# Gate and up products of six of eight token blocks as seven half-size products, with four FFN banks and a down product taken pair by pair

## Chip, cores and metric

One NeuronCore of a Trainium2 chip runs the whole program. The metric is device time in microseconds (us), as the median of several executions. Profiles are one execution each, recorded by the hardware profiler.

## What is computed

The input x has 4 sequences of 1024 tokens with 512 channels. The reference does this (weights come as arguments, `ternary` rounds a matrix to -1, 0, 1 times its mean magnitude):

```
xn  = layernorm(x)
# attention: 16 heads of 32, decayed linear attention in chunks of 128 tokens
q, k, v = split(rmsnorm(xn, qkv_norm_w) @ ternary(qkv_w).T)
per chunk:  o = scale * ((q k^T * mask) v + (q * lam_t) S);  S = lam_T * S + (k * lam_rev)^T v
att = rmsnorm(rmsnorm(o, norm_w), proj_norm_w) @ ternary(proj_w).T
# FFN, hidden size 2048
ffn = (silu(xn @ w_gate.T) * (xn @ w_up.T)) @ w_down.T
out = x + att + ffn
```

## The kernel before

The 4096 tokens are cut into eight blocks b = 0 to 7 of 512 tokens. Every float32 factor of a product is split into two float16 halves, hi and lo, and a product is the sum of hi·hi, hi·lo and lo·hi, so each product of 128 contracted channels costs three matmuls (with exact ternary weights only two).

The FFN of a block works on the hidden size in 16 slices j of 128, in two halves of 8 slices. `ffn_up` makes one slice: for gate and then for up, 4 channel groups times 3 matmuls with 512 moving columns (tokens), 12 matmuls into one PSUM bank of pool `ps_f` (3 banks). ScalarE (ACT) takes the silu of the gate bank (line 852); VectorE (DVE) multiplies the up bank with it (line 855); ACT rounds the result to its hi half (line 879), and GpSimd (POOL), or DVE for the last slices of a half, makes the lo half (line 880). Two slices share one tile `ghl` and one scale, and are called a pair below. After 8 slices, `ffn_down` makes the four token chunks one after the other, each with 24 matmuls of 512 columns into one bank, with down weights that stay in SBUF (tiles `wda` and `wdb`). DVE adds the bank to `acc` (line 905). Gate and up weights are converted to hi and lo once, in block 0, kept in DRAM as `gu_d`, and read again in each later block, 512 KB for a slice, four slices ahead (`load_gu`).

Block 0 has another loop (`ffn0`), in which the weights are converted while they are used.

The attention of a block is made in two halves of 256 tokens (`att_half`), a coroutine with some 30 yields. In its course: four steps of q and k products (16 matmuls of 256 columns with the weights `wqkT`), two of v, then eight steps with scores (4 matmuls, into one of the two banks of pool `ps_s`, evicted by DVE in line 680, split by ACT in 684 and POOL in 685), the products with v four steps later (`intra`, evicted by ACT in 702 and DVE in 704), the state S (DVE, 732 and 739), norms (among them line 770 on DVE), and the projection.

The main loop has 48 steps for each block. In a step it issues one FFN piece (in blocks 1 to 7, 12 matmuls of 512 columns, 2.6 us of TensorE), then one yield of each attention half under way, then the pieces that `later(...)` has put down for this step: a list FIRST, which runs at the head of a step, and a list LAST, which runs at its end. `in_order` chains the instructions of DVE, ACT, POOL and SyncE (SP) in this written order, so that each of those engines works strictly through its list; TensorE's (PE's) order is the program's as well. `ln_plan` puts the layernorm of block b+1 into the last third of block b: loads, statistics, scaling on ACT, then the hi half on ACT, the lo half on POOL (line 479) and a transposing DMA into `xT`, four of them for a block. `place` picks the step of a few loads by how many bytes are due around it. All but one small DMA are issued by SP, in one queue.

Of the kernel before, what the change touches and what calls it, by code (L numbers as in the profile page):

```python
# [20 lines left out]
XS = 2.0**10  # L21
# [7 lines left out]
def block_kernel(ctx, tc, x, qkv_w, qkv_nwT, proj_w, proj_nwT, proj_nw, norm_w, s, w_gu, w_down, out):  # L29
# [17 lines left out]
    ps_f = ctx.enter_context(tc.tile_pool(name="ps_f", bufs=3, space=bass.MemoryType.PSUM))  # L47
    ps_s = ctx.enter_context(tc.tile_pool(name="ps_s", bufs=2, space=bass.MemoryType.PSUM))
# [92 lines left out]
    gu_d = dram.tile([P, NJ * 2048], F16, tag="gu_d", name="gu_d")  # L141
# [9 lines left out]
    ones = pnw_bc[:, :P]  # L151
# [9 lines left out]
    def t32():  # L161
        return wt([P, 512], F32, "t32", 10)
# [46 lines left out]
    def load_x(c, tag="xin", bufs=4):  # L209
        xt = wt([P, C], F32, tag, bufs)  # L210
        SY.dma_start(xt, xf[c * P : (c + 1) * P, :])
        return xt
# [50 lines left out]
    def tern_scale(src, count, col):  # L263
        n = len(src)
        a = asum[:, col : col + n]
        for i in range(n):
            with after(pin):
                sumabs(i, src[i], a[:, i : i + 1])
            if i % 2:
                yield  # L270
        r1 = ct([P, 1], F32, f"r1_{col}")
        V.tensor_reduce(r1, a, AX.X, ALU.add)
        yield
        yield
        sc = tsc[col]
        V.tensor_scalar(sc[:, 0:1], col_sums(r1, 1), 1.0 / count, 1e-5, ALU.mult, ALU.max)
        V.tensor_scalar(sc[:, 1:2], sc[:, 0:1], 0.5, None, ALU.mult)
        V.tensor_scalar(sc[:, 2:3], sc[:, 0:1], -0.5, None, ALU.mult)
# [58 lines left out]
    def raw_pair(g, kind):  # L337

        if kind == 2:
            return [t32(), t32()]  # L340
        if g == 0 and kind == 0 or g % 2:
            t = wt([P, 2, C], F32, *(("ghl", 4) if g else ("kn", 1)))
            return [t[:, 0, :], t[:, 1, :], t]
        return [wt([P, C], F32, *(("xin", 4) if g else ("xn2", 2))) for _ in range(2)]
# [29 lines left out]
    def group_scale(g, kinds=(0, 1, 2)):  # L374


        m = gq.pop((g, kinds))
        o = om[:, g, kinds[0] : kinds[-1] + 1]
        oi = o.bitcast(I32)
        V.tensor_scalar(o, col_sums(m, len(kinds)), 2.0**-64, 2.0, ALU.max, ALU.mult)  # L380
        V.tensor_scalar(oi, oi, 24, 23, ALU.logical_shift_right, ALU.logical_shift_left)
        V.tensor_scalar(oi, oi, -1.0, float(204 << 23), ALU.mult, ALU.add)
        gs = slice(g, g + 1)
        if 0 in kinds:
            inverse(ug[:, gs], o[:, 0:1], 1 / XS)
            V.tensor_scalar(bsc0[:, gs], o[:, 0:1], 2.0**-30 / XS, None, ALU.mult)
        if 2 in kinds:
            V.scalar_tensor_tensor(cg[:, gs], om[:, g, 1:2], om[:, g, 2:3], bsc0[:, gs], ALU.mult, ALU.mult)
            inverse(icg[:, gs], cg[:, gs], 1 / XS)

# [4 lines left out]

    def group_conv(g, r, kinds=(0, 1, 2)):
        j = 2 * g + r
        if 0 in kinds:
            gu0[j] = gu = wt([P, 2, 2, CC, P], F16, "gu", 4)
        for kind in kinds:  # L400
            src, w1 = raw.pop((g, kind, r)), om[:, g, kind : kind + 1]
            if kind < 2:
                hi, lo = (gu[:, kind, n].rearrange("p c q -> p (c q)") for n in range(2))
            else:
                if g not in wd:
                    wd[g] = wd_tile(g // (NG // 2))
                hi, lo = (wd[g][:, r, n, :] for n in range(2))
            la = A.activation(hi, src, AF.Copy, scale=w1)
            if kind == 0 or g == 0 and kind == 1 or g <= 1 and kind == 2:
                lv = V.scalar_tensor_tensor(lo, src, w1, hi, ALU.mult, ALU.subtract)  # L410
            else:
                if kind == 1:
                    G.tensor_scalar(src, src, w1, None, ALU.mult)  # L413
                else:
                    A.activation(src, src, AF.Copy, scale=w1)
                lg[0] = G.tensor_tensor(lo, src, hi, ALU.subtract).ins  # L416
        if 0 in kinds:
            SY.dma_start(gu_d[:, j * 2048 : (j + 1) * 2048], gu.rearrange("p a b c d -> p (a b c d)"))
            return la.ins, lv.ins
# [15 lines left out]
    def ln_stats0():  # L435
# [16 lines left out]
        G.tensor_scalar(rs[:, 2, :], rs[:, 1, :], QS, None, ALU.mult)  # L452
# [21 lines left out]
    def ln_chunk(b, k):  # L474
        xts = lnst[b][1]
        xT = blk[b][0]
        xn2 = wt([P, 2 * C], F16, "xn2", 2).rearrange("p (a c) -> p a c", a=2)
        A.copy(xn2[:, 0, :], xts[k])  # L478
        G.tensor_tensor(xn2[:, 1, :], xts[k], xn2[:, 0, :], ALU.subtract)  # L479

        def turn():
            SY.dma_start_transpose(
                xT[:, :, :, k * P : (k + 1) * P].rearrange("p a c t -> p (a c) t"),
                xn2.rearrange("p a c -> p (a c)"),
            )

        return turn

    def ln_plan(b, end):
# [37 lines left out]
        def split(k):  # L527
            if k == 0:
                blk[b] = [wt([P, 2, CC, HB], F16, "xT", 1), None, rs]
            turns[k] = ln_chunk(b, k)  # L530

        turns = {}
        first, lo = b == 1, 0
        for k in range(4):
# [3 lines left out]
            else:  # L538
                lo = place(max(lo, e - 12), e, 0.7, lambda k=k: load(k))
            later(end - (10 - k // 2 if first else 18 - k), lambda k=k: stats(k), last=True)  # L540
            later(end - (6 - k // 2 if first else 12 - k), lambda k=k: scaled(k), last=True)
            later(end - ((5, 5, 3, 3) if first else (9, 8, 5, 4))[k], lambda k=k: split(k), last=True)
            later(end - ((4, 4, 2, 2) if first else (7, 6, 4, 3))[k], lambda k=k: turns[k]())
# [23 lines left out]
    def att_half(b, half):  # L567
        _, h, rs = blk[b]
# [52 lines left out]
        for k in range(2):  # L621
# [6 lines left out]
            vhl = wt([P, 2 * C], F16, "vhl", 5).rearrange("p (h a d) -> p h a d", a=2, d=D)  # L628
# [119 lines left out]
        def norms(u):  # L748
# [5 lines left out]
            o2, u.o3 = t32(), t32()  # L754
# [19 lines left out]
            if u.g < B * N // P - 2:  # L774
                on = wt([P, 2 * C], F16, "vhl", 5).rearrange("p (a c) -> p a c", a=2)
                oT = wt([P, 2 * C], F16, "vhl", 5).rearrange("p (a c t) -> p a c t", a=2, t=P)
# [64 lines left out]
    def ffn_up(b, j, gu, bs, done):  # L841
        xT = blk[b][0]
        xhi, xlo = xT[:, 0], xT[:, 1]
        for kind in range(2):
            pm = bank(ps_f)
            for c in range(CC):
                T.matmul(pm, gu[:, kind, 0, c, :], xhi[:, c, :], start=(c == 0), stop=False)
                T.matmul(pm, gu[:, kind, 0, c, :], xlo[:, c, :], start=False, stop=False)
                T.matmul(pm, gu[:, kind, 1, c, :], xhi[:, c, :], start=False, stop=(c == CC - 1))
# [3 lines left out]
            else:  # L853
# [4 lines left out]
                if b or j >= NJ - 4:  # L858
                    later(1, lambda: load_gu(NJ * b + j + 4))
            yield  # L860

    def load_gu(q):

        if q >= NB * NJ:
            return
        j = q % NJ
        gus[q] = gu = wt([P, 2, 2, CC, P], F16, "gu", 4)
        SY.dma_start(gu.rearrange("p a b c d -> p (a b c d)"), gu_d[:, j * 2048 : (j + 1) * 2048])

    gus = {}  # L870

    def plain(gts, late=NJ):


        def done(j, gf):
# [4 lines left out]
            (V if j > late else G).tensor_tensor(ghl[:, 1, :], gf, ghl[:, 0, :], ALU.subtract)  # L880
# [3 lines left out]
    def ffn_down(b, k, g0, gts, c):  # L884
# [29 lines left out]
    def load_acc(b, k):  # L914
        g = 4 * b + 2 * k
        acc[g // 2] = wt([P, 2, C], F32, "acc", 4)
# [3 lines left out]
    def ffn(b):  # L920
        for hh in range(2):
            js = range(hh * NJ // 2, (hh + 1) * NJ // 2)
            gts = []
            done = plain(gts, js[-4])
            for j in js:
                yield from ffn_up(b, j, gus.pop(NJ * b + j), bsc, done)
            for k in range(4):
                yield from ffn_down(b, k, js[0] // 2, gts, c2[:, hh : hh + 1])

    def ffn0():  # L930
        prev = None

        def down(ks):
            g, gts = prev
            for k in ks:
                for _ in ffn_down(0, k, g, gts, icg[:, g : g + 1]):
# [56 lines left out]
    masks((0, 1))  # L993
# [10 lines left out]
    def prep():  # L1004
        with after(pin):
            masks((2, 3))
        qw = load_rows(qkv_w, ("qst", "kst", "qhl", "khl"))
        SY.dma_start(nw_bc, norm_w.partition_broadcast(P))
        yield from prep_qkv_w(qw)

    def prep_proj():
        pw = []
        for r in range(2):
            t = wt([P, 2, C], F32, "acc", 4)
            SY.dma_start(t, proj_w[2 * r * P : 2 * (r + 1) * P, :].rearrange("(n p) c -> p n c", p=P))
            pw += [t[:, 0, :], t[:, 1, :]]
# [11 lines left out]
    mh.update({at[2 * b] + 7: (b, 1) for b in range(NB)})  # L1028
# [3 lines left out]
    for n in at:  # L1032
        for i, size in ((2, 1.3), (3, 2.0), (4, 1.3), (5, 2.0), (6, 4.0), (24, 2.0), (25, 2.0)):
            moved[n + i] = moved.get(n + i, 0) + size
    for b in range(1, NB):
        for i in range(0, TS, 2):
            if i % 24 < 16:
                moved[t0[b] + i] = moved.get(t0[b] + i, 0) + 1.3
        for i in (7, 6, 4, 3):
            moved[t0[b] - i] = moved.get(t0[b] - i, 0) + 2.0  # L1040
        for k in range(2):
            lo = max(at[2 * b - 2] + 12, t0[1] + 9) + k
            place(lo, max(lo + 4, t0[b] + 12), 1.3, lambda b=b, k=k: load_acc(b, k))
    side, side2 = prep(), prep_proj()
    t = 0
    for b in range(NB):
        if b + 1 < NB:
            ln_plan(b + 1, TS)
        for i, _ in enumerate(ffn(b) if b else ffn0()):
            for _ in range(int(0.8 * t) - int(0.8 * (t - 1))):  # L1050
                next(side, 1)
            if t == 12 or 28 <= t < 34 or 36 <= t < 56 and t % 2:
# [15 lines left out]
            if b == 0 and i == TS - 1:  # L1068
                half_scales(0)
                half_scales(1)  # L1070
                in_order(keep=False)
            run_due(FIRST)
# [59 lines left out]
```

## Time and profile before

| | |
|---|---|
| median of 3 executions | 1350.65 us (1350.37 to 1351.06) |
| profiled execution, its own time | 1351.69 us |
| its span, first to last instruction | 1348.7 us |
| busy, share of the span | PE 98%, DVE 52%, ACT 41%, POOL 46% |
| mean granted clock of PE | 0.997 |
| DMA | 178.10 MB, mean 132 GB/s; main queue busy for 47.9% of 16 engines' span |

The page names instruction groups by line, engine, operation, output and inputs, with the count, the busy time in us, the mean duration of one in ns, and after the bar the idle time of the engine just before them. Matmuls overlap each other, so the mean duration of one (381 ns for 512 columns) is its latency; what a matmul costs in a stream is the distance from one to the next, which is read from the timeline. A busy time with such overlap is a little over the sum of the distances.

### The profile page before, as it was taken

To read this page: it belongs to the slowest core of one execution; us is meant where nothing else is said; L and a number is where in the kernel's file an instruction comes from. 1 tells how busy PE (TensorE), PEld (TensorE's weight loads), DVE (VectorE), ACT (ScalarE), POOL (GpSimd) and SP (SyncE) were. 2 spreads that over 40 slices of the span, in tenths; PEclk is the share of its full clock that TensorE was granted. 3 is DMA by queue.
4 is the path that set the end of the run, shared out by engine and by line. 5 is a ranking of instruction groups with operands and counts; after the bars stand their busy time and mean duration, and the time that the engine had idled before them with its cause. 6 is when DMAs were issued, how large, how long until landed. Compare 5 with 4: busy or idle time off the path is not lost.

```text
span 1348.7 us, 21547 instructions
## 1 busy us (share of the span) xinstructions
PE 1318.9 (98%) x8514; PEld 695.3 (52%) x8514; DVE 701.0 (52%) x1228; ACT 557.0 (41%) x1061; POOL 619.1 (46%) x648
## 2 busy tenths in 40 slices
PE   4999999999999999999999999999999999999998
PEld 2444555555555555554555555554555555555554
DVE  7898744546343553537443364545534445446442
ACT  5846544244433344334433244433524235344341
POOL 3656753355424454435544254534635244544351
PEclk9999999999999999999999999999999999999999
DMA  9644637156371736335463636445372636444420
GB/s 342 244 155 149 187 90 198 59 148 148 89 194 32 187 95 168 114 102 129 101 170 95 157 110 134 116 123 129 94 171 88 156 102 157 104 130 112 110 63 32
DMA packets 156037, 178.10 MB, mean 132 GB/s; under 512 B 101664, under 2 KB 101664, under 8 KB 155936
## 3 DMA queue, kind: packets, MB, share of 16 engines
q1 hardware_dynamic: 155792, 176.73, 47.9%
q8 instruction: 66, 1.08, 0.3%
q14 instruction: 35, 0.29, 0.1%
q10 hardware_dynamic: 144, 0.01, 0.0%
HBM read 119.55 MB, written 33.55 MB: 114 GB/s over the span
## 4 chain that ended last, share of the span: by engine, by line
PE 88%; DVE 5%; DMA 2%; POOL 2%; issue 1%; ACT 1%; POOLq 0%; DVEq 0%; ACTq 0%; SPq 0%
PE psf L112 65%; PE psa L112 20%; PE pss L112 2%; DMA gu_d<-gu 1%; DVE acc L905 1%; DVE gs L366 1%; DMA xin<-in_x_dram 1%; DVE h L562 0%; POOL gu L416 0%; POOL ghl L413 0%; DMA t<-in_w_down_dram 0%; DMA xin<-in_w_gu_dram 0%; DVE t L288 0%; POOL xin L413 0%; DVE t L855 0%
## 5 line engine op out<-in xcount | busy, mean ns | idle before, releaser
L112 PE MATMUL psf<-xT,gu 128*128 128x512 f16 x3072 | 704.9, 381 | 5.8 <-DVE t L855 2.8
L112 PEld LDWEIGHTS <-gu 128*128 128x128 f16 x3072 | 294.6, 98 | 334.1 <-issue 11.0
L685 POOL TENSOR_TENSOR t<-t,t 128x512 f16<-128x512 f32 x128 | 150.5, 1177 | 186.5 <-ACT t L684 186.1
L112 PEld LDWEIGHTS <-ghl 128*128 128x128 f16 x1536 | 146.9, 98 | 163.6 <-issue 1.6
L880 POOL TENSOR_TENSOR ghl<-t,ghl 128x512 f16<-128x512 f32 x86 | 101.8, 1183 | 222.4 <-ACT ghl L879 221.9
L879 ACT CAST ghl<-t 128x512 f16<-128x512 f32 x128 | 79.0, 617 | 285.6 <-DVE t L855 285.5
L112 PE MATMUL psf<-wdb,ghl 128*128 128x512 f16 x768 | 175.5, 379 | 1.7 <-DVE acc L905 1.0
L112 PE MATMUL psf<-wda,ghl 128*128 128x512 f16 x768 | 175.7, 379 | 0.0
L855 DVE SCALAR_TENSOR_TENSOR t<-psf,bsc,t 128x512 f32<-128x512 f32 x128 | 95.9, 749 | 123.1 <-PE psf L112 114.4
L852 ACT ACTIVATE t<-psf,ug 128x512 f32<-128x512 f32 x128 | 87.5, 684 | 123.4 <-PE psf L112 123.2
L680 DVE SCALAR_TENSOR_TENSOR t<-pss,rs,mask 128x512 f32<-128x512 f32 x128 | 95.5, 746 | 77.7 <-PE pss L112 73.9
L684 ACT CAST t<-t 128x512 f16<-128x512 f32 x128 | 78.8, 616 | 115.4 <-DVE t L680 114.8
L112 PE MATMUL psa<-h,wqkT 128*128 128x256 f16 x1024 | 122.2, 273 | 1.4 <-DVE S L732 1.4
L112 PEld LDWEIGHTS <-wqkT 128*128 128x128 f16 x1024 | 99.8, 98 | 25.4 <-issue 1.6
L905 DVE SCALAR_TENSOR_TENSOR acc<-psf,c,acc 128x512 f32<-128x512 f32 x56 | 42.1, 751 | 69.1 <-PE psf L112 68.9
L644 POOL TENSOR_TENSOR t<-t,t 128x512 f16<-128x512 f32 x28 | 33.5, 1198 | 79.2 <-ACT t L643 79.1
L781 POOL TENSOR_TENSOR vhl<-t,vhl 128x512 f16<-128x512 f32 x30 | 35.5, 1182 | 64.7 <-ACT vhl L780 64.6
L112 PEld LDWEIGHTS <-t 128*128 128x128 f16 x1040 | 47.6, 96 | 32.1
L631 DVE SCALAR_TENSOR_TENSOR vhl<-psa,rs,vhl 128x512 f16<-128x512 f32 x32 | 24.0, 751 | 74.8 <-ACT vhl L630 68.6
L112 PE MATMUL psa<-wvT,h 128*128 128x512 f16 x256 | 60.5, 379 | 1.3 <-DVE S L732 1.3
L479 POOL TENSOR_TENSOR xn<-xin,xn 128x512 f16<-128x512 f32 x28 | 32.7, 1169 | 59.3 <-ACT xn L478 59.1
L706 POOL TENSOR_TENSOR t<-t,t 128x512 f32<-128x512 f32 x28 | 38.8, 1385 | 45.8 <-DVE t L704 45.8
(202 smaller groups left out, 1402.7 us busy)
## 6 DMA issues: line engine op xcount, KB each, us to landing
gu<-gu_d SPq DMA_DIRECT2D x112, 512.0 KB, 3.7
qst<-sd SPq DMA_DIRECT2D x48, 256.0 KB, 4.3
kst<-sd SPq DMA_DIRECT2D x48, 256.0 KB, 4.4
xin<-in_x_dram SPq DMA_DIRECT2D x32, 256.0 KB, 4.4
acc<-in_x_dram SPq DMA_DIRECT2D x16, 512.0 KB, 4.8
gu_d<-gu SPq DMA_DIRECT2D x16, 512.0 KB, 4.0
sd<-qhl SPq DMA_DIRECT2D x16, 512.0 KB, 2.9
sd<-khl SPq DMA_DIRECT2D x16, 512.0 KB, 3.5
```

The lines of the kernel that those rows point to most:

```text
L112: tc.keep_in_program_order(nc.tensor.matmul(*a, **k))
L644: G.tensor_tensor(vrl, vr, vrh, ALU.subtract)
L680: V.scalar_tensor_tensor(sm, pss, u.rk, mask[:, 4 * qd : 4 * qd + 4, :], ALU.mult, ALU.mult)
L684: A.copy(smh, sm)
L685: G.tensor_tensor(sml, sm, smh, ALU.subtract)
L706: later(1, lambda: G.tensor_tensor(u.o, u.o, u.oc, ALU.add), last=True)
L781: G.tensor_tensor(on[:, 1, :], u.o3, on[:, 0, :], ALU.subtract)
L852: pa = A.activation(sl, pm, AF.Silu, scale=ug[:, j // 2 : j // 2 + 1])
L855: pv = V.scalar_tensor_tensor(gf, pm, bs[:, j // 2 : j // 2 + 1], sl, ALU.mult, ALU.mult)
L879: A.copy(ghl[:, 0, :], gf)
L880: (V if j > late else G).tensor_tensor(ghl[:, 1, :], gf, ghl[:, 0, :], ALU.subtract)
L905: V.scalar_tensor_tensor(acc_of(g), ps, c, acc_of(g), ALU.mult, ALU.add)
```

## The change

Blocks 0 and 1 keep the old way of making gate and up. In blocks 2 to 7 (the third to the eighth), the gate matrix of a pair of slices (256 hidden by 512 channels) and the block's xn (512 channels by 512 tokens) are each cut into four quarters, and the product is made from seven products of quarters or sums of quarters in place of eight. Each product is 128 hidden by 256 channels by 256 tokens, that is 2 channel groups times 3 matmuls of 256 columns. `up_seven` issues them in four steps for a pair: four products of gate, four of up, three of gate, three of up. After four products DVE adds parts of the two banks (`sums`), and the three later products are accumulated on top of the same banks. The same is done with up.

- `ps_f` has four banks, `ps_s` one.
- The sums of weight quarters are made in block 1 (`up_sums`: loads, four subtractions or additions of 256 columns on POOL, the split on ACT and DVE, stores to `gu_d`). A pair then reads four parts, two of 512 KB and two of 384 KB, in place of two slices of 512 KB.
- The sums of token quarters are made with the layernorm of the next block (`sums` in `ln_plan`, on POOL): two more tiles, T12 and T34, each split on ACT and POOL and turned by two DMA transposes, so eight transposes for a block in place of four.
- `ffn_down` goes pair by pair with all four token chunks in four banks at once; in blocks 2 to 7 the down weights come from a copy in DRAM (`wd_d`, stored in block 1), 512 KB for a pair. The matmuls are the same in number and shape.
- The lo half of a pair's result is always made on POOL. The x tiles share the float32 tiles `t32` (16 in place of 10); `vhl` and `xn2` share `x16` (7); `acc` has three tiles. The loads and the conversion of the projection weights move from steps 12 to 56 to steps 44 to 56. At the start, the two POOL multiplications of `masks((0, 1))` stand after the layernorm's small POOL operations.

```diff
-    ps_f = ctx.enter_context(tc.tile_pool(name="ps_f", bufs=3, space=bass.MemoryType.PSUM))
-    ps_s = ctx.enter_context(tc.tile_pool(name="ps_s", bufs=2, space=bass.MemoryType.PSUM))
+    ps_f = ctx.enter_context(tc.tile_pool(name="ps_f", bufs=4, space=bass.MemoryType.PSUM))
+    ps_s = ctx.enter_context(tc.tile_pool(name="ps_s", bufs=1, space=bass.MemoryType.PSUM))
...
+        def sums(k):
+            (b11, b21), (b12, b22) = ([xts[i][:, f * UT : (f + 1) * UT] for f in range(2)] for i in (k, k + 2))
+            t12, t34 = ts_[k] = [t32() for _ in range(2)]
+            for dst, x, y in (
...
+                G.tensor_tensor(dst, x, y, ALU.subtract)
...
+    def up_seven(b, g, gts):
...
+        def prod(dst, w, x, fresh=False):
+            for c in range(2):
+                for m, n in ((0, 0), (0, 1), (1, 0)):
+                    T.matmul(dst, w[:, m, c, :], x[:, n, c, :], ...
...
+        for kind in range(2):
+            w = parts7.pop((q, kind))
+            pa, pb = (bank(ps_f, (P, 2, UT)) for _ in range(2))
+            for i, dst in enumerate((pa[:, 0], pa[:, 1], pb[:, 0], pb[:, 1])):
+                prod(dst, w[:, i], x4[i], fresh=i % 2 == 0)
+            u = halves_of(t32())
+            us.append((pa, pb, u))
+            A.copy(u[:, 0], pa[:, 0])
+            def sums(pa=pa, pb=pb, u=u):
+                V.tensor_tensor(u[:, 0], pa[:, 1], u[:, 0], ALU.add)
+                V.tensor_tensor(u[:, 1], pb[:, 0], u[:, 0], ALU.add)
+                V.tensor_tensor(u[:, 1], pb[:, 1], u[:, 1], ALU.add)
+            later(1, sums, lambda kind=kind: load_next(2 * NJ + 3 * q + kind + 4))
+            yield
...
+        for kind in range(2):
+            w = parts7.pop((q, 3 - kind))
+            pa, pb, u = us[kind]
+            for i, dst in enumerate((pa[:, 0], pb[:, 0], pb[:, 1])):
+                prod(dst, w[:, i], x3[i])
+            def sums(pb=pb, u=u):
+                v = halves_of(t32())
+                V.tensor_tensor(v[:, 1], pb[:, 0], u[:, 0], ALU.add)
+                V.tensor_tensor(u[:, 0], pb[:, 1], u[:, 0], ALU.add)
...
+            def times(dst, src, by):
+                V.scalar_tensor_tensor(dst, src, scale[1], by, ALU.mult, ALU.mult)
+            if kind == 0:
+                later(1, sums, gate, lambda: load_last(q + 2))
+                later(1, gate_rest, last=True)
+            else:
+                later(1, sums, lambda pa=pa: times(sl[3][:, 0], pa[:, 0], sl[1][:, 0]))
+                later(1, lambda: times(sl[2], sl[2], sl[0]), lambda: times(sl[3][:, 1], sl[3][:, 1], sl[1][:, 1]), last=True)
...
+                later(2, high, last=True)
+                later(3, low, last=True)
+            yield
...
+    def ffn_down(b, hh, gts, c):
+        pd = [None] * 4
+        for n, t in enumerate(gts):
+            w = wd[g] if b == 1 else wdn.pop((b, g))
+            for k in range(4):
...
+                if end:
+                    later(1, lambda k=k: add_acc(b * 4 + k, pd[k], c))
+                if k % 2:
+                    yield
```

## Prediction

> **What bounds the kernel now.** I read the page's busy shares and its chain first, then the groups, then the timeline of PE, DVE and POOL, then the DMA rows.
>
> ```profile
> PE 1318.9 (98%) x8514; PEld 695.3 (52%) x8514; DVE 701.0 (52%) x1228; ACT 557.0 (41%) x1061; POOL 619.1 (46%) x648
> PE 88%; DVE 5%; DMA 2%; POOL 2%; issue 1%; ACT 1%; POOLq 0%; DVEq 0%; ACTq 0%; SPq 0%
> L112 PE MATMUL psf<-xT,gu 128*128 128x512 f16 x3072 | 704.9, 381 | 5.8 <-DVE t L855 2.8
> ```
>
> PE is busy almost throughout, and the chain that ended last lies on it. The gate and up products are over half of its work, and it idled only 5.8 us before them. So a matmul less is time less, until another engine is late. The timeline of PE shows what a matmul costs in a stream:
>
> ```profile
> 434.85 1.91 PE L112 MATMUL psa<-h,wqkT 128*128 128x256 f16 x16
> 436.59 2.75 PE L112 MATMUL psf<-xT,gu 128*128 128x512 f16 x12
> 439.18 1.04 PE L112 MATMUL psa<-h,wqkT 128*128 128x256 f16 x8
> ```
>
> Starts, not durations, count: 12 of 512 columns take 439.18 - 436.59 = 2.59 us, 0.2162 each; 16 of 256 columns take 1.74 us, 0.1088 each, with a weight load for every one.
>
> **What PE saves.** Per pair and kind (gate or up), 24 matmuls of 512 columns (5.19 us) become 42 of 256 (4.57 us): 0.62 us less. Six blocks, eight pairs, two kinds are 96 times: 59.6 us. Down keeps its matmuls, the attention too. If 256 columns cost what busy time over count gives (122.2 / 1024 = 0.119 us), only 18 us would be saved; but that counts tails that overlap the next group, so I take the starts.
>
> Here a rule speaks against the change. The row first: the 16 matmuls above load 16 times, 98 ns each, and still follow at 0.1088 us, so the loads lie under the products before them, with 10 ns to spare. The Trainium skill, "TensorE: Matmul & The Clock Gate", section "The mechanism", says that weight loads overlap matmuls in flight only where the row groups differ, and these all use full rows. By that rule the 18 more loads for each of the 96 would cost 18 x 98 ns x 96 = 169 us, and the kernel would be some 110 us slower. This trace disagrees with it, and the sum goes by the row.
>
> **What DVE pays.** These are its rows:
>
> ```profile
> L704 DVE TENSOR_TENSOR t<-psa,t 128x256 f32<-128x256 f32 x64 | 26.8, 419 | 16.9 <-ACT t L702 16.5
> L770 DVE SCALAR_TENSOR_TENSOR t<-t,sq,pnw_bc 128x512 f32<-128x512 f32 x32 | 34.0, 1062 | 0.0
> L562 DVE SCALAR_TENSOR_TENSOR h<-t,nwT,h 128x256 f16<-128x256 f32 x64 | 42.2, 700 | 4.3 <-ACT h L561 4.2
> 442.37 1.65 DVE L770 SCALAR_TENSOR_TENSOR t<-t,sq,pnw_bc 128x512 f32<-128x512 f32 x1
> 442.31 1.16 POOL L781 TENSOR_TENSOR vhl<-t,vhl 128x512 f16<-128x512 f32 x1 [0.29 <-ACT vhl L780]
> ```
>
> The first is the new sum exactly (256 columns, PSUM and SBUF). The last two show that a DVE operation with both inputs in SBUF sits while POOL works: L770 takes 0.741 us at its shortest, 1.648 at its longest, 1.062 on average; L562 0.472 to 1.391, 0.700 on average. The multiplications by silu (`times`) are now of that kind, since two of three sums lie in SBUF. A pair costs DVE 10 sums x 0.419 + one `times` from PSUM (between L704's 0.42 and L855's 0.75; 0.45, since it has L704's size) + 1.06 + 0.70 = 6.4 us, 51 us for a block. Before, 16 x 0.749 (L855) + 6 x 0.768 (lo halves on DVE) = 16.6 us. DVE goes from about 82 to 118 us of a block that gives PE about 157: not the bound on average. But it follows a written order, and the banks come round. Each kind has two of the four banks, so the FFN piece of a step needs the sums of two steps before; and those stand in DVE's queue behind the attention's evictions of that earlier step. What DVE owes for a step it must finish within PE's next step, or PE waits, and with it the attention's matmuls queued behind on PE, for whose results DVE then waits. The single score bank adds the same: scores need the eviction (L680, 0.746) of the step before. That one comes first in its step on DVE and has the 2.0 to 2.6 us of an FFN piece to finish in, so alone I cost it at nothing; without that cover, a step would cost up to 0.75 us.
>
> I laid the built program's DVE operations, step by step, at the rows' durations, against PE's. Eight score steps in the second half of block 4 (steps 28 to 35): PE has two pairs (18.3 us), scores 1.8, products with v 0.9, state 0.7: 21.6 us. DVE has 20 sums 8.4, `times` 4.4, scores 6.0, statistics of the next block 3.5, state 2.05, two L704 0.8, a small one 0.2: 25.3 us. Queued operations overlap by 0.08 us where the next does not need the one before (in the timeline L905 to L680, L631 to L637), which leaves about 23. So DVE is 1.5 to 4 us over. About 1.5 us of slack lies in the order of the products (the first writes a quarter that ACT freed; the quarters that DVE must free come 0.65 and 1.3 us later), except where three products of up end: there `times` frees the first bank last. Over the 13 halves whose scores fall into blocks 2 to 7 (some beside down, where no sums are due; half of them without the statistics) this gives 0.5 us each with overlap and slack, 2.7 with neither: 7 to 35 us. I take 1.5 each, 20 us, since queued DVE rows do overlap.
>
> **ACT, POOL, block ends.** ACT gets a copy (367 ns, L702) for each kind; its work per block goes from 68 to 78 us, covered. POOL gets per block 8 subtractions of 256 columns (half of L685's 1.18, so 0.6 each; 1.18 at most), four more lo halves of layernorm (1.17 each, L479), and the six that DVE made: 74 to about 92 us of 157. It is behind near a block's end: in step 40 of block 4 it holds 6.4 us against PE's 2.6. Behind it stand the transposing DMAs on SP, and behind those on SP the weight parts and the attention's spreads, which PE needs in the next block's first steps. The turns start 8 steps (some 25 us) before, and a transpose lands in 3.1 us, so mostly this is covered; uncovered it is up to POOL's lag of 5 us a block. Between 0 and 30 us; I take 5, since only the last turns are close. Block 1 has `up_sums` (POOL 64 x 0.6, DVE 32 x 1.06, ACT 32 x 0.71): DVE 116 and POOL 113 us against PE's 165, covered.
>
> **Loads.** A pair reads 1.8 MB of parts for 1.05 before, and 0.5 MB of down weights: 63 MB more over 48 pairs. The DMA share is 0.48 at some 125 GB/s in the middle of the trace and 0.96 at 345 GB/s in the first 36 us; 63 MB at the latter's rate add 0.18 over 950 us, to 0.66. Parts are issued four steps ahead (10 us) and land in 3.7 us (gu row); twice that would still be hidden. If they were late by the whole landing time, each of 48 pairs would cost up to 3.7 us. I cost them at nothing.
>
> **The start.** The chain of the first 13 us passes through a mask multiplication:
>
> ```profile
> 9.25 1.24 POOL mask L199
> ```
>
> PE's first transposes wait there for DVE's L447, which waits for POOL's roots behind the masks. Masks moved behind the roots give up to two of these, 2.5 us; or nothing, as DVE is busy with line 366 from 21 to 29 us anyway. I take 2. The projection weights move beside steps where DVE has room: 0.
>
> **The sum.** 1351.69 (profiled execution) - 59.6 - 2 + 20 + 5 = 1315.1. The median of the runs lies 1.04 us under the profiled execution: 1314.
>
> **Rivals.** (a) DVE's slack suffices everywhere. For it: PE idled 5.8 us before all gate and up products of the trace. Against it: the 25.3 against 21.6. Stalls 3 us, block ends 3: 1351.7 - 59.6 - 2 + 6 - 1 = 1295. (b) Block ends are not covered: POOL's lag and the row of transposes hold the first products of six blocks 5 us each, 30 for my 5: 1339. For it: the 6.4 against 2.6. Against it: eight steps of lead. (c) The other side: DVE becomes the bound of all up steps, because POOL, now busy for some 60% of the time, holds the two `times` in SBUF. At their longest they take 1.65 and 1.39, 1.28 us more for a pair, 61 us over 48 pairs. It decides from 59.6 / 48 = 1.24 us of stall per pair on. With half of the 61 on top of 35, block ends 5: 1351.7 - 59.6 - 2 + 65 + 5 - 1 = 1359. For it: PE cannot run ahead of DVE by more than two steps. Against it: in the down steps, a third of all, DVE catches up. (d) The halved matmuls are not worth what the columns say (0.119): with the stalls, 1356. Against it: the starts.
>
> **Chances.** Forecast 0.56, (a) 0.15, (b) 0.14, (c) 0.13, (d) 0.02. The forecast's own range, with 7 to 35 for DVE and 0 to 12 at block ends, is 1296 to 1336. The whole range, 1296 to 1346, takes in (b), leaves out half of (a) and most of (c). About 0.2% (2.7 us) is what a measurement of this kernel can tell from no change: faster 0.85, same 0.02, slower 0.13.
>
> **What would show it.** In the profile after: psf matmuls of 256 columns with starts 0.109 us apart; DVE near 118 us of a block; PE's idle time named as `sums` or `times` lines (DVE, psf), about 20 us, in score steps and not in down steps; a few us for xT or wda behind DMA at block starts. The forecast is wrong if PE's idle time names the weight parts or `pss`, if 256-column starts lie 0.12 us or more apart, or if the DVE waits exceed 60 us.

## The result, and the profile after

The changed kernel takes 1361.95 us (median of 4 executions, 1361.29 to 1362.66), the kernel before 1350.86 beside it. The ratio is 1.0081 (95% interval 1.0064 to 1.0099): 0.8% slower, where 1314 had been forecast. The profiled execution has a span of 1359.5 us against 1348.7.

From the page of the changed kernel: busy time and instructions, the main DMA queue, the chain that ended last.

```profile
PE 1279.5 (94%) x10242; PEld 868.5 (64%) x10242; DVE 921.2 (68%) x1752; ACT 622.7 (46%) x1261; POOL 783.1 (58%) x820
q1 hardware_dynamic: 229680, 266.92, 69.1%
PE 64%; DVE 19%; POOL 8%; issue 4%; ACT 3%; DMA 2%; SPq 0%; DVEq 0%; POOLq 0%; ACTq 0%
```

PE works less and still ends later. The chain that ended last ran on PE for 88% of the span before; now it does for 64%, and DVE and POOL together hold 27% of it. What PE does became cheaper about as forecast. From the timeline of PE after:

```profile
481.25 2.13 PE L112 MATMUL psf<-wda,gu 128*128 128x256 f16 x18
483.21 0.39 PE L112 MATMUL pss<-qst,kst 96*128 96x128 f16 x4
```

18 matmuls of 256 columns in 1.96 us are 0.109 us each, with a weight load for every one.

To place the loss, I compared the distance between the starts of successive steps in each trace with that step's matmuls at their distances (0.2162 for 512 columns, 0.1088 for 256). What a step took beyond that is called its loss below. Over blocks 1 to 7, PE's work is 59.4 us less after by this count, and the loss rose from 3.6 to 74.4 us. The first 48 steps end 1.0 us sooner, the tail is 0.4 longer: -59.4 - 1.0 + 70.8 + 0.4 = 10.8, the difference of the spans. So the question is what the 70.8 us are. What PE waited for, by the view of waits after (us, times, longest; lines that are about as long in the view before, and small ones, are left out):

```profile
PE psf L112 <- DVE t L966: 18.2, 17, 2.2
PE psf L112 <- DVE t L983: 15.7, 15, 2.9
...
PE pss L112 <- DVE t L710: 9.1, 5, 4.0
PE psf L112 <- DVE acc L1108: 4.4, 3, 2.7
...
PE psf L112 <- DMA gu_d<-x: 2.9, 1, 2.9
...
PE pss L112 <- DMA gu<-gu_d: 2.4, 1, 2.4
```

L966 is the first of the three sums after four products, L983 the last of the two after three products, L710 the score eviction. The transfers, in spite of 90 MB more traffic, are not the story: the two DMA lines are 5.3 us.

The 74.4 us lie in two places. The steps with gate and up products (up steps) of blocks 2 to 7 lost 55.8 us, for 1.5 before; the down steps of all blocks lost 18.7 us, for 1.9 before.

### The profile page after: what moved, and what is told of

Read it like the earlier page. It is cut to its first block, busy times and chain, and to the rows that moved or that the text cites. A ratio compares the mean times of both kernels' runs of the same rounds, so it can differ in the third digit from the quotient of the medians.

```text
span 1359.5 us, 26534 instructions
## 1 busy us (share of the span) xinstructions
PE 1279.5 (94%) x10242; PEld 868.5 (64%) x10242; DVE 921.2 (68%) x1752; ACT 622.7 (46%) x1261; POOL 783.1 (58%) x820
## 3 DMA queue, kind: packets, MB, share of 16 engines
q8 instruction: 80, 1.31, 0.4%
## 4 chain that ended last, share of the span: by engine, by line
PE 64%; DVE 19%; POOL 8%; issue 4%; ACT 3%; DMA 2%; SPq 0%; DVEq 0%; POOLq 0%; ACTq 0%
PE psf L112 46%; PE psa L112 17%; DVE t L994 2%; DVE h L592 2%; DVE t L710 2%; DVE acc L1108 1%; PE pss L112 1%; POOL ghl L1013 1%; POOL t L715 1%; POOL x L489 1%; DVE S L762 1%; POOL t L541 1%; DVE t L967 1%; DVE t L983 1%; DVE t L966 1%
## 5 line engine op out<-in xcount | busy, mean ns | idle before, releaser
L112 PEld LDWEIGHTS <-gu 128*128 128x128 f16 x3936 | 380.8, 98 | 154.2 <-issue 26.6
L112 PE MATMUL psf<-xT,gu 128*128 128x256 f16 (+1 forms) x1920 | 333.8, 317 | 16.3 <-DVE t L983 5.7
L112 PE MATMUL psf<-wdb,ghl 128*128 128x512 f16 x1344 | 310.2, 381 | 3.6 <-DVE t L983 2.9
L112 PE MATMUL psf<-wda,gu 128*128 128x256 f16 x2016 | 245.5, 273 | 7.3 <-DVE t L983 7.2
L710 DVE SCALAR_TENSOR_TENSOR t<-pss,rs,mask 128x512 f32<-128x512 f32 x128 | 95.5, 746 | 52.1 <-PE pss L112 51.2
L112 PEld LDWEIGHTS <-wda 128*128 128x128 f16 x864 | 85.3, 100 | 38.8 <-issue 22.8
L112 PE MATMUL psf<-xT,wda 128*128 128x256 f16 x576 | 81.3, 279 | 18.8 <-DVE t L966 15.8
L811 POOL TENSOR_TENSOR x<-t,x 128x512 f16<-128x512 f32 x30 | 35.6, 1186 | 85.0 <-ACT x L810 85.0
L994 DVE SCALAR_TENSOR_TENSOR t<-t,bsc,t 128x512 f32<-128x512 f32 x96 | 72.8, 799 | 0.3
L1009 ACT CAST ghl<-t 128x512 f16<-128x512 f32 x96 | 55.2, 617 | 34.3 <-DVE t L994 34.3
L489 POOL TENSOR_TENSOR x<-t,x 128x512 f16<-128x512 f32 x52 | 61.2, 1182 | 14.4 <-ACT x L488 14.3
L661 DVE SCALAR_TENSOR_TENSOR x<-psa,rs,x 128x512 f16<-128x512 f32 x32 | 24.0, 750 | 62.2 <-ACT x L660 62.2
```

The source lines that it names most:

```text
L112: tc.keep_in_program_order(nc.tensor.matmul(*a, **k))
L489: G.tensor_tensor(xn2[:, 1, :], src, xn2[:, 0, :], ALU.subtract)
L710: V.scalar_tensor_tensor(sm, pss, u.rk, mask[:, 4 * qd : 4 * qd + 4, :], ALU.mult, ALU.mult)
L811: G.tensor_tensor(on[:, 1, :], u.o3, on[:, 0, :], ALU.subtract)
L994: V.scalar_tensor_tensor(dst, src, scale[1], by, ALU.mult, ALU.mult)
L1009: A.copy(ghl[:, :, 0, cols], t)
```

## Experiments

Times are medians of 2 to 8 executions. The kernel before ran beside each of them and had 1350.58 to 1350.64. I call "stretch" what DVE's instructions took beyond the durations of their groups' fast tenth, summed from 160 us to 1345 us: 44.3 us before, 90.6 after. Blocks are counted from 0, but in the expectation on lo halves by a copy from 1.

### Four first edits of the changed kernel

**Sums in the step itself, ahead of the attention's evictions**

```diff
-            later(1, sums, lambda kind=kind: load_next(...))
+            sums()
+            later(1, lambda kind=kind: load_next(...))
...
-                later(1, sums, gate, lambda: load_last(q + 2))
+                sums()
+                later(1, gate, lambda: load_last(q + 2))
...
```

> Three theories for the 70 us that PE lost beside the forecast. Hold: DVE's operations with both inputs in SBUF stretch while POOL works without a break (90.6 us over their shortest durations after, 44.3 before), and POOL works 783 us now. Amount: DVE simply has too much work in the up steps (921 us busy, 701 before). Order: DVE has the time, but the sums of a step stand in its queue behind the attention's evictions of that step, so that the banks come free late. Here the sums are issued in the step itself, ahead of the attention's work on DVE; nothing else moves. Order: the 34 us that PE waits for L966 and L983 go, 1325 to 1335. Hold and amount: the same work comes out in another order, the wait moves from the FFN banks to the score bank and the attention, 1350 to 1368.

Measured 1348.98 (ratio to before 0.9989, interval 0.9972 to 1.0006): 13 us better, more than hold or amount gave, less than order did. One line of its waits shows where the rest went:

```profile
PE pss L112 <- DVE t L710: 34.6, 23, 4.0
```

L966 fell to 0.6 us, and the score bank's wait rose from 9.1 to 34.6. The sums no longer come late; the scores do, which now stand behind them.

**Lo halves by a copy on ACT**

```diff
-                        G.tensor_tensor(ghl[:, :, 1, cols], t, ghl[:, :, 0, cols], ALU.subtract)
+                        A.copy(ghl[:, :, 1, cols], t)
```

> The lo halves of silu times up in blocks 3 to 8 are made by a copy on ACT instead of a subtraction on POOL (the subtraction of the hi half is left out). 96 instructions of 1.2 us, 115 us, leave POOL; 96 of some 0.6 us, 59 us, come to ACT (623 us busy so far); DVE's list is untouched. Hold: DVE's excess over its shortest durations falls from 90.6 to about 50 to 65 us, and the time to 1320 to 1335. Amount: DVE does as many operations as before, 1352 to 1362. Order: the same as amount.

Measured 1349.80 (ratio 0.9991, 0.9980 to 1.0002). POOL fell from 783 to 673 us, the stretch from 90.6 to 76.9. The 12 us gained are less than half of what hold asked for, and more than the others allowed. The waits for L966 even rose, from 18.2 to 20.7.

**One sum less**

```diff
-                V.tensor_tensor(u[:, 1], pb[:, 0], u[:, 0], ALU.add)
-                V.tensor_tensor(u[:, 1], pb[:, 1], u[:, 1], ALU.add)
+                V.tensor_tensor(u[:, 1], pb[:, 1], u[:, 0], ALU.add)
```

> One of the three DVE sums of each half with four products is left out (one product is not added): 96 instructions of 0.425 us, 41 us of DVE, with one input in PSUM, so of the kind that POOL does not stretch. POOL's list is untouched. Amount: nearly all of it returns as time where DVE is the bound, two thirds of the steps and more: 1322 to 1335. Hold: the stretched operations stay, but the queue behind them is shorter: 1338 to 1350. Order: the banks come free 0.43 us sooner in 96 halves, 34 us of waits fall by a half: 1342 to 1350. Beside the run with lo halves on ACT it says what a microsecond of DVE is worth against one of POOL.

Measured 1354.58 (ratio 1.0029, 1.0009 to 1.0048). DVE did 40 us less, and the time fell by 7. Amount asked for 27 or more, so it falls. Hold and order had said 1350 at most, so both miss too, by 4.6 us. The waits for L966 were 20.8 (18.2 in the changed kernel), for the last sum 12.6 (15.7). What PE waits for is the first of the sums, and taking a later one away does not bring the first forward.

**No sums of weight quarters**

```diff
-                SY.dma_start(gu_d[:, g, kind, n]..., ts_[r][:, f]...)
...
-        load()
-        later(2, sums, last=True)
+                SY.dma_start(gu_d[:, g, kind, n], gu_d[:, g, kind, ((0, 4), (7, 5))[r][f]])
...
-            later(3 + r, lambda r=r: split(r), last=True)
```

> The sums of weight quarters for the later blocks are left out: their places in memory are filled with copies of raw quarters, by transfers alone, at the same steps. DVE loses 32 operations of 0.74 to 4.99 us, POOL 64 of 0.77, ACT 32, all in the blocks 1 and 2 (from 0), where PE lost 7.5 and 14.6 us. Hold and amount: block 1 gains up to 7, block 2 up to 8 us of it: 1346 to 1354. If their place in the first two blocks costs nothing, as the prediction had it: 1360 to 1363.

Measured 1349.06 (ratio 0.9986, 0.9974 to 0.9997), 13 us better. The loss in block 1 went from 7.5 us to nothing, in block 2 from 14.6 to 10.4, and the waits for the score eviction L710 fell from 9.1 us to 1.6. The prediction had this work in block 1, "covered"; of its sixteen groups five in fact start in block 2 (which begins with step 96), the last at step 112, and three in the last ten steps of block 1, beside the layernorm of block 2.

### Where in DVE's list the sums stand

The first run left one question: is it DVE's amount after all, which reappears in the score bank, or is there a place that serves both? A step issues its FFN piece, then the attention's pieces, then LAST; the sums stood in FIRST of the next step, so behind LAST.

**The score bank by itself, on the kernel before**

```diff
-    ps_f: bufs=3, ps_s: bufs=2
+    ps_f: bufs=4, ps_s: bufs=1
```

> The kernel before with four FFN banks and one bank for scores, and nothing else of the change. It tells what the single score bank costs by itself, with DVE as little busy as before (701 us). If the bank alone costs, as an eviction of 0.75 us in each of the 13 x 8 score steps would have it: up to 78 us, 1365 to 1430. If, as the prediction had it, the FFN piece covers the eviction: 1349 to 1354. In the second case the 9 to 35 us of waits for L710 in the runs so far come from what stands ahead of L710 on DVE, not from the bank.

Measured 1350.22 beside 1350.58 (ratio 0.9996, 0.9985 to 1.0007). PE waited 2.1 us for the score eviction (L680), in two places. The bank is free when DVE comes in time. The edit adds a fourth FFN bank as well; what that gains by itself was not tested.

**Sums between the attention's evictions and the rest of the step**

```diff
-            later(1, sums, lambda kind=kind: load_next(...))
+            mid.append(sums)
+            later(1, lambda kind=kind: load_next(...))
...
-                later(1, sums, gate, lambda: load_last(q + 2))
+                mid.append(sums)
+                later(1, gate, lambda: load_last(q + 2))
...
-                later(1, sums, lambda pa=pa: times(sl[3][:, 0], pa[:, 0], sl[1][:, 0]))
+                mid.extend((sums, lambda pa=pa: times(sl[3][:, 0], pa[:, 0], sl[1][:, 0])))
...
                 if next(hf, 1) == 1:
                     halves.remove(hf)
+            while mid:
+                mid.pop(0)()
             run_due(LAST)
```

> The sums (and the multiplication from PSUM) are put between the two kinds of attention work on DVE: behind the step's score eviction and the other evictions of its attention piece, ahead of the rest of the step (statistics of the next block, h, the attention's norms). With the sums in the step itself, ahead of the scores, the run gave 1349 and its waits went to L710 (34.6 us). Order: both banks come free in time, L966, L983 and L710 together fall from 43 to under 20 us: 1335 to 1345. Hold and amount: no better than with the sums ahead of the scores, 1347 to 1356.

Measured 1330.33 (ratio 0.9850, 0.9821 to 0.9879): 31.6 us better than the changed kernel, 20 better than before, and below even the range that order gave. The counts of instructions on each engine are those of the changed kernel: nothing is taken away. The same stretch of block 3 in both kernels; first the changed kernel:

```profile
629.06 0.69 DVE L507 BATCH_NORM_STATS2 st<-t 128x6 f32<-128x512 f32 x1
...
629.85 0.39 PE L112 MATMUL pss<-qst,kst 96*128 96x128 f16 x4
...
630.07 0.88 DVE L592 SCALAR_TENSOR_TENSOR h<-t,nwT,h 128x256 f16<-128x256 f32 x2
...
630.88 0.42 DVE L982 TENSOR_TENSOR t<-psf,t 128x256 f32<-128x256 f32 x1
...
631.33 0.42 DVE L983 TENSOR_TENSOR t<-psf,t 128x256 f32<-128x256 f32 x1
...
631.80 0.82 PE L112 MATMUL psf<-xT,gu 128*128 128x256 f16 x6 [1.18 <-DVE t L983]
```

and then this one, where the two sums are lines 983 and 984:

```profile
623.07 0.41 DVE L983 TENSOR_TENSOR t<-psf,t 128x256 f32<-128x256 f32 x1
623.09 0.39 PE L112 MATMUL pss<-qst,kst 96*128 96x128 f16 x4
...
623.51 0.42 DVE L984 TENSOR_TENSOR t<-psf,t 128x256 f32<-128x256 f32 x1
...
623.99 0.81 PE L112 MATMUL psf<-xT,gu 128*128 128x256 f16 x6
...
624.25 0.68 DVE L507 BATCH_NORM_STATS2 st<-t 128x6 f32<-128x512 f32 x1
...
625.07 0.85 DVE L592 SCALAR_TENSOR_TENSOR h<-t,nwT,h 128x256 f16<-128x256 f32 x2
```

In the changed kernel, statistics of the next block (L507) and h of the next half (L592) stand ahead of the two sums. Nobody needs them soon: in this trace no other engine waited for an L592. But PE sits for 1.18 us. Here the sums run first, and PE's piece follows its predecessor. Of the waits over the whole run, those for the score eviction, the first and the last sum:

```profile
PE pss L112 <- DVE t L710: 17.8, 14, 4.0
...
PE psf L112 <- DVE t L966: 3.0, 4, 1.4
PE psf L112 <- DVE t L984: 2.8, 3, 1.2
```

Together they are 23.6 us, from 43.0; order had asked for under 20. The loss beyond PE's work is 42.6 us, where it was 74.4. Nearly all of the difference lies in the up steps of blocks 2 to 7 (22.9 us, from 55.8), while the down steps keep theirs (19.7, from 18.7). DVE is busy for 909 us, where it was 921, and the stretch is 82.3, from 90.6; so neither the amount nor the stretch is enough for these 32 us.

**The weight sums earlier**

```diff
-    sums_at = [t0[1] + 8 + 15 * i // 4 for i in range(2 * NG)]
+    sums_at = [t0[1] + 2 + 11 * i // 4 for i in range(2 * NG)]
```

> The run before, with the sixteen sums of weight quarters from 2 to 43 steps after the start of block 1 (from 0) instead of 8 to 64, so that none is left in block 2. Leaving the weight sums out gave 13 us (block 1 lost 7.8 us less, block 2 lost 4 less). Where the crowding of block 2 was the price, 3 to 6 us less than the run before; where it only moves to block 1, where DVE has less to do per step, the same within 3 us. Order with both: 1330 to 1342; hold and amount: 1344 to 1356.

Measured 1338.07 (ratio 0.9907, 0.9879 to 0.9936), 8 us worse than the run before. Block 1 lost 17.9 us in its down steps for 7.8; block 2 gained 4. The time is in order's range, but both statements on the place miss: in block 1 they are not the same as elsewhere but worse. Closer together they meet the layernorm of block 2 more often, which is argued from the steps only.

**Three edits together**

```diff
+            mid.append(sums)
...
+                        A.copy(ghl[:, :, 1, cols], t)
...
+                SY.dma_start(gu_d[:, g, kind, n], gu_d[:, g, kind, ((0, 4), (7, 5))[r][f]])
```

> Three edits together: sums between scores and the rest, lo halves copied on ACT (their subtraction is left out), no sums of weight quarters (raw quarters are copied instead). Alone, lo on ACT gave 12 us and no weight sums 13. If the losses are separate (hold in the up steps, crowding in blocks 1 and 2, order of the queue), the gains add: 1362 - 12 - 13 - 13 or more = 1324 or less. If they are one and the same, a queue on DVE that any relief shortens until the next thing is late, the sum is less than 30: 1332 to 1342. In either case the floor is the prediction's case with enough slack, 1295 to 1300.

Measured 1310.10 (ratio 0.9700, 0.9672 to 0.9728): 52 us below the changed kernel, where the three alone gave 31.6, 12.2 and 12.9, 57 in all. So most of each is separate. The kernel leaves out the lo subtractions and the weight sums, so this is a bound and not a version to use. The loss beyond PE's work is 21.6 us.

### What POOL's work does

**Weight sums around the end of block 1**

```diff
-    sums_at = [t0[1] + 8 + 15 * i // 4 for i in range(2 * NG)]
+    sums_at = [t0[1] + (2 + 7 * i // 2 if i < 10 else 19 + 3 * i) for i in range(2 * NG)]
```

> The kernel with the sums between scores and the rest (1330.3), with the sixteen sums of weight quarters placed around the end of block 1 (from 0) instead of across it: ten from 2 to 33 steps after its start, six from 1 to 16 steps into block 2. The run with all of them in block 1 had lost 17.9 us in the down steps of block 1, against 7.8. If it is the meeting of the weight sums with the next block's layernorm at the end of block 1 that costs, those 7.8 us go and block 2 keeps its own: 1322 to 1327. If any place is as bad as another, 1328 to 1335.

Measured 1328.37 (1326.40 to 1329.39; ratio to before 0.9835, 0.9822 to 0.9849). The down steps of block 1 lost 2.2 us for 7.8, most of what was expected; the time is above the range given, since block 2 lost 1.1 more, block 5 1.3 more. It is 2 us under 1330.33, which the two intervals do not tell apart. Of the versions that leave nothing out it is the fastest, and it beats both kernels.

**Lo halves on ACT, with the sums in place**

```diff
-                        G.tensor_tensor(ghl[:, :, 1, cols], t, ghl[:, :, 0, cols], ALU.subtract)
+                        A.copy(ghl[:, :, 1, cols], t)
```

> The kernel with the sums between scores and the rest (1330.3), and the lo halves of silu times up copied on ACT, as before (the subtraction is left out). POOL has 115 us less to do, DVE's list is the same. With both this and no weight sums the run gave 1310.1. Hold: POOL's share of what is left (42.6 us over PE's work) is 10 to 14 us here as it was 12 before: 1316 to 1321. If the order of the queue was all, and POOL does not matter once DVE's sums come in time: 1327 to 1331.

Measured 1324.45 (ratio 0.9806, 0.9788 to 0.9824), 5.9 us under 1330.33 and between the two ranges. Of 7.0 us less loss, 4.2 lie in the down steps of block 3, at the block's end.

**POOL's lo halves made twice, on the kernel before**

```diff
-            (V if j > late else G).tensor_tensor(ghl[:, 1, :], gf, ghl[:, 0, :], ALU.subtract)
+            for _ in range(1 if j > late or late == NJ else 2):
+                (V if j > late else G).tensor_tensor(ghl[:, 1, :], gf, ghl[:, 0, :], ALU.subtract)
```

> The kernel before, with every lo half that POOL makes in blocks 1 to 7 subtracted twice in a row (same values): some 90 more operations of 1.2 us on POOL, 619 to 725 us, none on DVE. It asks by itself whether POOL's work stretches DVE's. Hold: DVE's busy time rises by 10 to 30 us without an instruction more, in the operations with both inputs in SBUF (44.3 us over their shortest durations before), while those with an input in PSUM keep theirs; the time stays within 5 us, since DVE has room there: 1350 to 1356. If POOL does not hold DVE, DVE's busy time stays at 701 within 3 us.

Measured 1350.44 (ratio 1.0001, 0.9991 to 1.0011). From its page:

```profile
PE 1316.8 (98%) x8514; PEld 694.9 (52%) x8514; DVE 702.8 (52%) x1228; ACT 556.4 (41%) x1061; POOL 706.7 (52%) x718
```

70 operations more than before, and POOL works 88 us more; DVE works 1.8 us more (stretch 46.6 for 44.3). So hold as a rate, more POOL hence slower DVE, falls. It takes a meeting: of the 204 DVE instructions in the trace before that have two inputs in SBUF and 256 columns or more, 89 began while an instruction of POOL ran, and these hold all of this group's stretch, 42.1 us; the other 115 hold none. In this run 94 began so. The extra subtractions met hardly any.

**No sums of token quarters, with the sums in place**

```diff
-            t12, t34 = ts_[k] = [t32() for _ in range(2)]
+            t12, t34 = ts_[k] = xts[k], xts[k + 2]
...
-                G.tensor_tensor(dst, x, y, ALU.subtract)
+                pass
```

> The kernel with the sums between scores and the rest (1330.3), with the subtractions of token quarters on POOL left out (raw quarters go on instead; their ACT halves and transposes stay): 48 operations of some 0.75 us, 37 us of POOL at the ends of blocks 1 to 6, just ahead of the transposes. The prediction put 5 us on block ends. If POOL's lag there is what holds the first products of the next block, it gives the losses of the last down steps and first up steps of blocks 2 to 6, 6 to 9 us: 1321 to 1325. If the transposes or the layernorm ahead of them hold, nothing: 1328 to 1331.

Measured 1319.33 (ratio 0.9768, 0.9751 to 0.9786): 11.0 us less for 36 us of POOL. The loss falls by 5.6 us in the down steps of block 1 and by 4.2 in those of block 3; the up steps keep theirs. So the sums of token quarters, POOL's work ahead of the transposes at the ends of blocks, cost 11 us. The edit also takes four `t32` tiles fewer in each block; what that is worth by itself was not tested.

## Why the prediction was wrong

**PE saves 59.6: right.** The distance of 0.109 us held in the new stream, with the loads under the products. One figure was read a little high: 2.59 us over 12 matmuls are 0.2158 us each and not 0.2162, and with 0.2158 and 0.109 the saving is some 58 us. The rule that the prediction took from the Trainium skill ("TensorE: Matmul & The Clock Gate", "The mechanism"), that loads overlap matmuls only where the row groups differ, does not hold in these traces; the 169 us estimated by it are not there. The same section also lets a load be pulled ahead when it goes to the background weight buffer, which the prediction left out, so these rows speak against its "only" and not against the whole section.

**DVE's stalls, 20 us: the failing step.** The costs of the work were good: sums 415 to 425 ns for the predicted 419, and these groups for 450, 1060 and 700:

```profile
L994 DVE SCALAR_TENSOR_TENSOR t<-psf,bsc,t 128x256 f32<-128x256 f32 x48 | 22.8, 475 | 0.0
L994 DVE SCALAR_TENSOR_TENSOR t<-t,bsc,t 128x512 f32<-128x512 f32 x48 | 46.7, 973 | 0.3
L994 DVE SCALAR_TENSOR_TENSOR t<-t,bsc,t 128x256 f32<-128x256 f32 x48 | 30.0, 625 | 0.0
```

Blocks 4 to 6 gave DVE 116 to 119 us for the predicted 118 (which the prediction's own terms, 82 - 16.6 + 51, put at 116 to 117). Two readings were off without weight in the sum: L770 took 0.720 us at its shortest, L562 1.396 at its longest.

What failed was the step from the balance of eight steps (25.3 against 21.6) to the stalls of the whole run. The balance treats DVE's time in a step as one sum. In those eight steps themselves the changed kernel lost 2.8 us, the upper end that the balance had given (2.7). But the score steps among all up steps of blocks 2 to 7 lost 35.0 us where I took 20, and the up steps without scores, which I put at nothing, lost 20.7: together 55.7 us in place of 20, where the kernel before lost 1.5. I wrote that the sums stand "behind the attention's evictions"; they stand behind LAST as well, behind work that is not due. The run that put them where the prediction had them, behind the evictions and ahead of LAST, lost 14.7 and 8.1 us in these two kinds of steps. So one move in the list was worth 31.6 us. That these 23 us come near the 20 of the sum is in part luck, since 8.1 of it lie in steps that I had put at nothing. A sum over steps says how much must be done, not what has to be done first. The 31.6 include what the clock adds: see below.

**`up_sums` covered in block 1: wrong, 14 us** (1324.45 to 1310.10 with it left out). My count of 116 us against 165 was an average over the block, and part of the work falls into block 2. The price of DVE's split, taken at 1.06 us, was right on average (1.04 us over its 32 instructions), but one of them sat for 4.99.

**Block ends 5 us: too small by half,** 11 us by the run without token sums, with POOL's work per block (89 to 95 us in blocks 4 to 6) as forecast at 92. "Eight steps of lead" covered some blocks and not 1 and 3, where the last down steps lose 7.7 and 4.2 us with the sums moved.

**The single score bank at nothing: right by itself** (1350.22), and right only under its condition: 34.6 us of waits appeared when sums went ahead of L710. **Loads: right,** with a DMA share of 0.69 for a predicted 0.66, though partly by luck: the traffic grew by 90 MB, where I had counted 63. **The start: 3.9 us gained at the first FFN step for 2,** of which block 0 gives 2.9 back.

**Where the 70.8 us went.** By the loss beyond PE's work, along the runs: the place of the sums 31.8 (74.4 to 42.6), lo halves on POOL 7.0 (to 35.6), weight sums 14.0 (to 21.6); 3.6 were there before. Some 18 us are left over the blocks. Of the 21.6, 8.3 lie in block 7 with its two attention halves 14 steps apart (3.5 of them there before); these I did not take apart. The 11 us of the token sums are no further item: 5.6 us at the end of block 1 go with the token sums, and also when the weight sums stand elsewhere, and 4.2 us at the end of block 3 go with the token sums, and also with the lo halves. There several works of POOL meet, and any one of them taken away relieves the place. Nor did I separate how much of POOL's 7.0 is its lag and how much its hold on DVE.

**The rivals.** (c) named 1359 and came nearest, but not by its mechanism: the two `times` from SBUF stretched by 18.1 us in all, 0.38 for a pair, where it needed 1.24, doubling POOL's lo halves left DVE alone in the kernel before, and taking them off POOL in the changed kernel gave 12 us. (b)'s mechanism exists at about a third of its price. (a) would need 1295; the three edits together reach 1310. (d) is excluded by 0.109. Of the signs of being wrong that the prediction had asked for, two were there: `pss` among the waits, and a transfer of weight parts (`gu<-gu_d`) for 2.4 us. The waits for DVE's sums, score evictions and `acc` came to 47 us by the view, under the 60 that it had set.

## What to carry to other kernels

Where an engine follows a written list, ask of every new wait what stands ahead of the awaited instruction, down to the slot of the step it is issued in; a fitting sum of durations does not help if work that is due in twenty steps stands ahead of work that is due now. An experiment that takes away work behind the awaited instruction (here 40 us for 7) and one that only moves it (31.6 us for nothing taken away) tell the two apart quickly. Work that is spread by a formula over steps should be laid over the places where the other planners put theirs: here that took 5.6 us from the end of block 1, of which 2 us showed in the time, within its noise.

## What the hardware showed that I had not expected

**A DVE instruction can sit through several of POOL's.** From the timeline after (start, duration):

```profile
328.65 1.15 POOL L715 TENSOR_TENSOR t<-t,t 128x512 f16<-128x512 f32 x1
328.69 4.99 DVE L1044 SCALAR_TENSOR_TENSOR x<-t,om,x 128x512 f16<-128x512 f32 x1
...
329.77 1.15 POOL L489 TENSOR_TENSOR x<-t,x 128x512 f16<-128x512 f32 x1
...
333.72 0.75 DVE L710 SCALAR_TENSOR_TENSOR t<-pss,rs,mask 128x512 f32<-128x512 f32 x1
334.34 1.53 POOL L1038 TENSOR_TENSOR t<-t,t 128x256 f32<-128x256 f32 x2
...
334.52 0.59 PE L112 MATMUL pss<-qst,kst 96*128 96x128 f16 x4 [3.96 <-DVE t L710]
```

L1044 has both inputs in SBUF and takes 0.74 us at its shortest. It began 0.04 us after a POOL instruction, and four of POOL's ended and a fifth began before it was done; the score eviction queued behind it cost PE 3.96 us. The Trainium skill, "SBUF — State Buffer", "SBUF: two separate sides", calls the port pair that the two engines share an exclusive lock, held for a whole instruction. This row agrees that one engine waits for the other. But waiting for the one POOL instruction that ran would have been 1.15 us, and the row shows 4.25 us beyond the shortest: the DVE instruction was not served between POOL's.

**The clock halves after waits shorter than I thought of.** PE ran at a granted clock of 0.5 for 24.0 us in the changed kernel (seven windows of 3.4 or 3.5 us), 9.7 before, 11.2 with the sums moved. Five of the seven windows lie in the steps of blocks 1 to 7, none before and one with the sums moved. The matmuls in these five took 7.8 us longer than at their usual distances, so some 8 us of the 70.8 are this, and some 6 of the 31.8 that the place of the sums gave. In the timeline:

```profile
1120.86 0.82 PE L112 MATMUL psf<-xT,gu 128*128 128x256 f16 x6 [0.16 <-DVE t L983]
...
1125.88 1.41 PE L112 MATMUL psf<-xT,wda 128*128 128x256 f16 x6 [2.24 <-DVE t L966]
1127.09 1.49 PE L112 MATMUL psf<-wda,wda 128*128 128x256 f16 x6
...
1226.65 1.47 PE L112 MATMUL psf<-wda,gu 128*128 128x256 f16 x12 [2.91 <-DVE t L983]
1227.96 0.39 PE L112 MATMUL pss<-qst,kst 96*128 96x128 f16 x4
```

From 1125.88 six matmuls take 1.21 us from start to start, for 0.65, after no wait longer than 2.24 us. The Trainium skill, "TensorE: Matmul & The Clock Gate", "Why this matters for your kernels", puts the limit at idle gaps of about 3 us; here 2.24 was enough. So a wait of PE of some 2 us can cost 1.7 us more. It need not: after the wait of 2.91 us at 1226.65, twelve matmuls take 1.31 us, full speed. The length of the wait alone does not decide; what does, these runs do not show.
